# Layer 0's product: ScalarE's quarter in moving blocks of 512 columns, projection one piece sooner

## The chip, the cores and the metric

The kernel runs on one core of a Trainium2 chip. A core has several engines with a queue each: TensorE (matrix products, written PE in the profile, its weight loads PEld), VectorE (DVE), ScalarE (ACT), GpSimd (POOL) and SyncE (SP, which only issues transfers here). They run side by side and wait for each other through semaphores. The metric is the device time of one execution, in microseconds (us). Three runs of the kernel before gave 768.58, 769.27 and 770.39 us, so the median is 769.27 us.

## The reference

The input x has 8 batches of 2048 nodes with 64 channels; adj is a 2048 x 2048 matrix over the nodes. There are two layers, each with a residual and a layer normalization. What matters here is layer 0, a graph convolution whose weights differ from node to node:

```python
w = jnp.einsum('nd,dkio->nkio', embedding, weight)      # d: 16, k: 3, i and o: 64
b = jnp.einsum('nd,do->no', embedding, bias)
As = [eye, A, 2.0 * (A @ A) - eye]
x_g = jnp.einsum('knm,bmc->bnkc', jnp.stack(As, 0), x)
out = jnp.einsum('bnki,nkio->bno', x_g, w)
return out + b
...
x = _layernorm(x + _L0_gnn_ref(x, adj, ...), axis=-1)
x = _layernorm(x + _L1_gnn_ref(x, adj, adj, ...), axis=-1)
```

Layer 1 is a second graph convolution with weights that all nodes share. It begins with a projection of the normalized output h of layer 0, and then multiplies by adj again.

## The kernel before, in words

The kernel goes through three large stages: two multiplications by adj that give the hop and the second hop of x (up to 227 us), layer 0's product with the normalization and the projection (227 to 534 us), and the multiplications by adj of layer 1 (the rest). Only the second of these is changed, with the loop that runs it (lines 834 to 867) and the function `mix0` (line 394).

**The tiles.** The 2048 nodes are 16 tiles of 128 nodes (`NT`, `P`). A tile has 512 columns: 8 batches by 64 channels. The loop over t handles layer 0's product of tile t, the operands for tile t + 1, and what follows for tile t - 1: its normalization and its projection.

**The product.** It swaps the order of the sums in the reference: TensorE first multiplies the features of a tile with `weight` for each embedding entry d, and the result is then scaled, node by node, with the embedding and summed over the 16 entries. A matmul takes as stationary operand the transposed features of one batch (64 channels by 128 nodes) and as moving operand the weights of four embedding entries (64 by 4 x 64 = 256 columns). Two batches lie on rows 0 to 63 and 64 to 127, and their matmuls follow each other as a pair. To keep float32 precision the features and the weights are split into a high, a low and a mixed part (`tt[k][n]`, `w_parts[n][k]`), so that with three k there are nine products to be summed per result.

The loop in `mix0` makes eight blocks per tile: g (two groups of four batches) by dg (four groups of `DG` = 4 embedding entries). A block is 2 x 3 x 3 x 2 = 36 matmuls into one `bank("pm")`, a tile of two PSUM banks. There are four such tiles (line 74), which pm, the transposes (pt) and the projection (pu) share in turn; the next user of one waits until its last reader is done.

**Taking the blocks out.** For six blocks VectorE does it: per embedding entry one `scalar_tensor_tensor` of 128 x 256 (line 431), which multiplies with the embedding column and adds to `acc`. For two blocks (dg = 0 of both g, a quarter of the tile) ScalarE does it: four `activation` of 128 x 256 (line 429) into the tile `aside`. GpSimd sums them in `summed` (line 403) and adds the sum to `acc` in `add_aside` (line 400). In the last tile ScalarE takes two blocks of each g (`on_act` = 2). `aside` comes from the pool `rawp` (five buffers), which also holds parts of the second hop.

**The work between the blocks.** The dictionary `at` says which work is issued ahead of which block (g, dg). Every engine works off its queue in the order of issue (`ordered`). The steps are:

- `of_x`, `of_hop`, `of_second` make the operands of tile t + 1 with `parts` (line 309), three steps each: the high part on ScalarE (line 312), the low part on VectorE (line 314), the mixed part on ScalarE and GpSimd (lines 319 and 320). `of_hop` begins with TensorE transposes (line 300). The input of `of_x` is loaded by SP in `operands` (line 702).
- n1, n2, n3 are the later steps of `layernorm` (line 359) of tile t - 1: square on ScalarE (line 353); square sums, variance (`ln_v`, line 334) and square root (`ln_sd`, line 336); then reciprocal root on VectorE (lines 339, 342, 343 and 345) and scaling on GpSimd (line 374). Ahead of them stand the sums, the mean and the subtraction (lines 362, 363, 365).
- `transpose(h, "hT")` and `project(t - 1, ...)` (line 443): eight transposes, and eight matmuls on `v`, whose results ScalarE copies to z (line 460).
- `times_r(t + 2)` scales the second hop on GpSimd (line 692), and `begin_sum(t + 1)` prepares the next `acc` on GpSimd (line 387).

In the last tile the first steps of layer 1 (`early`) take the place of the next tile's operands.

Of the kernel before, what the change touches and what calls it, by code (L numbers as in the profile page):

```python
# [9 lines left out]
F32 = mybir.dt.float32  # L10
# [3 lines left out]
AF = mybir.ActivationFunctionType  # L14
ALU = mybir.AluOpType
# [3 lines left out]
P = 128  # L19
B, N, C = 8, 2048, 64  # L20
NT = N // P
D = 16
DG = 4
# [16 lines left out]
def pattern(  # L40
# [22 lines left out]
    nc = tc.nc  # L63
# [7 lines left out]
    rawp = pool(ctx, "fraw", RAW)  # L71
# [12 lines left out]
    def bank(name):  # L84

        return psum.tile([P, 2, 512], F32, tag="ps", name=name)
# [40 lines left out]
    def ordered(ins):  # L127
        if in_order:
            tc.keep_in_program_order(ins)
# [173 lines left out]
    def transpose(src, tag, pt=None):  # L303

        tt = xcpool.tile([P, B // 2, P], F32, tag="ln_xc", name=tag)
        ordered(nc.scalar.copy(by_half(tt), transposed(src, pt)))
        return tt
# [75 lines left out]
    def begin_sum(t):  # L383

        acc = work.tile([P, B, C], F32, tag="acc", name="acc")
        for g in range(2):
            ordered(nc.gpsimd.tensor_tensor(
                acc[:, 4 * g : 4 * g + 4, :].rearrange("p (j i) c -> p j i c", j=2),
                bc(0, t)[:, 4 * g : 4 * g + 4, :].rearrange("p (i j) c -> p j i c", j=2),
                ebias[:, t : t + 1, :].unsqueeze(1).to_broadcast([P, 2, 2, C]), ALU.add,  # L390
            ))
        return acc

    def mix0(t, tt, acc, at, on_act=1):

        aside = [None, None]

        def add_aside(g):
            part = acc[:, 4 * g : 4 * g + 4, :]
            ordered(nc.gpsimd.tensor_tensor(part, part, aside[g][:, 0], ALU.add))  # L400

        def summed(one, other, n):
            ordered(nc.gpsimd.tensor_tensor(one[:, :n], one[:, :n], other, ALU.add))  # L403

        for g in range(2):
            part = acc[:, 4 * g : 4 * g + 4, :]
            for dg in range(D // DG):
                if (g, dg) == (1, 2 if on_act == 1 else 0):
                    add_aside(0)
                for work_here in at.get((g, dg), ()):  # L410
                    work_here()
                ds = slice(dg * DG, (dg + 1) * DG)
                pm = bank("pm").rearrange("p j (i d c) -> p j i d c", i=2, d=DG)
                for i in range(2):
                    for k in range(3):
                        for n in range(3):
                            for j in range(2):
                                q = slice(j * C, (j + 1) * C)
                                nc.tensor.matmul(  # L419
                                    pm[:, j, i], lhsT=tt[k][n][q, 2 * g + i, :], rhs=w_parts[n][k][q, ds, :],  # L420
                                    start=(k == 0 and n == 0), stop=(k == 2 and n == 2),
                                )
                if dg < on_act:
                    to = rawp.tile([P, DG, B // 2, C], F32, tag="raw", name="aside")
                for d in range(DG):
                    dd = dg * DG + d
                    got, e = pm[:, :, :, d, :].rearrange("p j i c -> p (j i) c"), emb_sb[:, t, dd : dd + 1]
                    if dg < on_act:
                        ordered(nc.scalar.activation(to[:, d], got, AF.Copy, scale=e))  # L429
                    else:  # L430
                        ordered(nc.vector.scalar_tensor_tensor(part, got, e, part, ALU.mult, ALU.add))  # L431
                if dg < on_act:
                    if dg == 0:
                        aside[g] = to
                    else:
                        summed(aside[g], to, DG)
                    if dg == on_act - 1:
                        for n in (2, 1):
                            summed(aside[g], aside[g][:, n : 2 * n], n)
        add_aside(1)  # L440
        return layernorm(acc)

    def project(t, hT, pus=None):


        for g in range(2):
            pm = bank("pu") if pus is None else pus[g]
            for i in range(2):
                for j in range(2):
                    q = slice(j * C, (j + 1) * C)  # L450
                    nc.tensor.matmul(  # L451
                        pm[:, j, i * 3 * C : (i + 1) * 3 * C], lhsT=hT[q, 2 * g + i, :], rhs=v[q],
                        start=True, stop=True,
                    )
            got = pm[:, :, : 6 * C].rearrange("p j (i k c) -> p j i k c", i=2, k=3)

            order = ["p (i j) c -> p j i c", "p (j i) c -> p j i c", "p (j i) c -> p j i c"]
            to = [bc(k, t)[:, 4 * g : 4 * g + 4, :].rearrange(order[k], j=2) for k in range(3)]
            for k in range(3):
                ordered(nc.scalar.copy(to[k], got[:, :, :, 2 - k, :]))  # L460
# [228 lines left out]
    def times_r(t):  # L689
        to = z2[:, t, :].rearrange("p (j n) -> p j n", n=P)  # L690
        r = rrow[:, t * P : (t + 1) * P].unsqueeze(1).to_broadcast([P, B // 2, P])
        ordered(nc.gpsimd.tensor_tensor(to, to, r, ALU.mult))  # L692
# [9 lines left out]
    def operands(t, quick=False):  # L702

        xt = work2.tile([P, B // 2, P], F32, tag="t0", name="xt")
        load(nc.sync, xt, xT[t])
        tt = [None] * 3

        def begin(k, src):
            where, tag = ((rawp, "raw"), (spool, "s"))[k != 2]
            high = hpool.tile([P, B // 2, P], F32R, tag="hl", name="hl")  # L710
            pair = where.tile([P, 2, B // 2, P], F32R, tag=tag, name="parts")
            tt[k] = [high, pair[:, 0], pair[:, 1]]
            return parts(src, tt[k], by_half if k == 1 else lambda to: to, quick)

        def of_x():
            yield from begin(0, xt)

        def of_hop(pt=None):
            yield from begin(1, transposed(z[1][t], pt))

        def of_second():
            yield from begin(2, by_pair(z[2][t]))

        return tt, of_x(), of_hop, of_second()
# [94 lines left out]
    def early(i, *kinds):  # L819

        got = third_got.setdefault(i, {})
        for lead, part in sorted(third[i], key=lambda part: -part[0]):
            if part.__name__ in kinds:
                part(got)
        third[i] = [part for part in third[i] if part[1].__name__ not in kinds]

    def go(it):
        return lambda: next(it)

    y, s = ("y_high", "y_low"), ("load_sum", "operands")  # L830
    acc, h, norm = first_tile[5], None, None
    tt = first_tile[0]
    coming = operands(1)
    for t in range(NT):
        got, last = {}, t == NT - 1
        at = {(g, dg): [] for g in range(2) for dg in range(D // DG)}
        n1, n2, n3 = [lambda: next(norm)] * 3 if t else [nothing] * 3

        if not last:
            following, of_x, of_hop, of_second = coming  # L840
            of_hop = of_hop()
            at[0, 1] += [go(of_x)] * (1 if t else 3)
            at[0, 2] += [go(of_hop), n1, go(of_hop), go(of_hop), n2]
            if t + 2 < NT:
                at[0, 2] += [lambda: times_r(t + 2)]
                at[1, 0] += [lambda: got.update(coming=operands(t + 2))]
            at[0, 3] += [n3, go(of_second), lambda: got.update(acc=begin_sum(t + 1))]
            at[1, 0] += [go(of_second), go(of_second)]
            at[1, 3] += [lambda: got.update(hT=transpose(h, "hT"))] if t else []
        else:  # L850
            at[0, 1] += [n1, lambda: early(0, *y, *s)]
            at[0, 2] += [n2, lambda: early(1, *y, *s)]
            at[0, 3] += [n3, lambda: early(2, *y)]
            at[1, 0] += [lambda: early(3, *y)]
            at[1, 1] += [lambda: early(4, *y)]
            at[1, 2] += [lambda: got.update(hT=transpose(h, "hT"))]
            at[1, 3] += [lambda: project(t - 1, got["hT"])]
        norm_now = mix0(t, tt, acc, at, 2 if last else 1)
        if 0 < t < NT - 1:
            project(t - 1, got["hT"])  # L860
        if "coming" in got:
            coming = got["coming"]
            next(coming[1])
            next(coming[1])
        norm = norm_now
        h = next(norm)
        if not last:
            tt, acc = following, got["acc"]
# [480 lines left out]
```

## Time and profile before

| what | value |
|---|---|
| median of three runs | 769.27 us |
| the profiled execution | 768.76 us, of which the span is 767.0 us |
| TensorE, matmul | 757.0 us busy, 99% |
| VectorE | 582.8 us busy, 76% |
| ScalarE | 387.7 us busy, 51% |
| GpSimd | 252.5 us busy, 33% |
| granted TensorE clock, mean | 0.997 |
| pm matmuls (line 419), 64 x 256 | 4608, 280 to 286 ns each as recorded |
| line 431, VectorE, 128 x 256 | 376, 483 ns each |
| line 429, ScalarE, 128 x 256 | 136, 475 ns each |
| lines 403 (GpSimd) | 66, 1068 ns each |

The span is the time from the first to the last instruction of the profiled execution. A row of the profile names the line, the engine, the operation, what it writes and reads, the shape and the count; then the busy time and the mean duration of one, and the idle time of the engine ahead of it with what ended that. The two matmuls of a pair run at the same time and matmuls overlap their neighbours, so their pace is read from how many end in a stretch and not from the recorded duration. The chain is the sequence of work that ended last, followed back from the end.

### The profile page before, as it was taken

How to read it: one execution, taken by the hardware profiler on the slowest of the kernel's cores; microseconds unless marked ns; L12 is line 12 of the kernel's file. 1: busy time of each engine (PE TensorE's matmuls, PEld its weight loads, DVE VectorE, ACT ScalarE, POOL GpSimd, SP SyncE). 2: the span in 40 equal slices, each digit the busy share in tenths (PEclk: the TensorE clock that was granted, in tenths of full speed). 3: DMA queues.
4: the chain of work that ended last, by engine and by line, in shares of the span. 5: the costliest groups of instructions: out<-in, count | busy, mean ns of one | idle time of the engine just before them, and what ended most of it. 6: DMA issues, size and time to landing. Idle time of an engine off the chain costs nothing.

```text
span 767.0 us, 18011 instructions
## 1 busy us (share of the span) xinstructions
PE 757.0 (99%) x7246; PEld 674.8 (88%) x7246; DVE 582.8 (76%) x1222; ACT 387.7 (51%) x760; POOL 252.5 (33%) x247
## 2 busy tenths in 40 slices
PE   8999999999999999999999999999999999999996
PEld 6888888888889999999999999998888888888886
DVE  6778766677758898888889888876688648668664
ACT  4446533878744555555545555547787763112111
POOL 0000000000026777777777777766100000012341
PEclk9999999999999999999999999999999999999998
DMA  8998996555510000000000000002354444565731
GB/s 308 374 389 294 340 313 209 164 168 164 171 60 27 20 8 19 20 17 16 17 16 10 20 17 3 3 29 70 127 168 146 138 149 137 178 183 164 217 128 45
DMA packets 73546, 96.77 MB, mean 126 GB/s; under 512 B 4848, under 2 KB 48368, under 8 KB 73328
## 3 DMA queue, kind: packets, MB, share of 16 engines
q1 hardware_dynamic: 62048, 76.66, 30.7%
q10 hardware_dynamic: 11408, 18.89, 6.6%
q8 instruction: 59, 0.97, 0.5%
q14 instruction: 31, 0.25, 0.1%
HBM read 76.65 MB, written 18.87 MB: 125 GB/s over the span
## 4 chain that ended last, share of the span: by engine, by line
PE 96%; DVE 2%; DMA 1%; ACT 1%; POOL 0%; issue 0%; SPq 0%; POOLq 0%; DVEq 0%
PE pm L419 35%; PE accT L641 27%; PE acc L254 15%; PE a L254 10%; PE accT L254 6%; PE pu L451 2%; DMA raw<-in_adj 1%; PE pt L300 1%; DVE acc L431 1%; PE accT L791 1%; DVE hl L238 0%; PE accT L451 0%; ACT aside L429 0%; SPq L123 0%; POOL xc L365 0%
## 5 line engine op out<-in xcount | busy, mean ns | idle before, releaser
L419 PE MATMUL pm<-wh,hl 64*128 64x256 f32 x1536 | 235.4, 286 | 0.7 <-DVE acc L431 0.7
L419 PE MATMUL pm<-wm,parts 64*128 64x256 f32 x1536 | 230.9, 280 | 0.0
L419 PE MATMUL pm<-wl,parts 64*128 64x256 f32 x1536 | 230.8, 280 | 0.0
L641 PE MATMUL accT<-s,hl 128*128 128x512 f32 x896 | 205.7, 390 | 0.0
L431 DVE SCALAR_TENSOR_TENSOR acc<-pm,pack_sb,acc 128x256 f32<-128x256 f32 x376 | 181.5, 483 | 27.5 <-PE pm L419 14.1
L641 PEld LDWEIGHTS accT<-s,hl 128*128 128x128 f32 x896 | 167.6, 188 | 35.4 <-issue 0.2
L419 PEld LDWEIGHTS pm<-wh,hl 64*128 64x128 f32 x1536 | 160.3, 188 | 1.2 <-PE pt L300 0.8
L419 PEld LDWEIGHTS pm<-wl,parts 64*128 64x128 f32 x1536 | 160.2, 188 | 0.0
L419 PEld LDWEIGHTS pm<-wm,parts 64*128 64x128 f32 x1536 | 160.0, 187 | 0.0
L629 ACT CAST s<-raw 128x1024 fp32r<-128x1024 bf16 x104 | 109.7, 1055 | 38.0 <-ACT hl L234 24.7
L254 PE MATMUL acc<-hl,s 128*128 128x512 f32 x512 | 117.3, 390 | 0.6 <-DVE s L223 0.6
L254 PEld LDWEIGHTS acc<-hl,s 128*128 128x128 f32 x512 | 95.8, 188 | 21.8 <-issue 1.0
L692 POOL TENSOR_TENSOR z<-z,rrow 128x512 f32<-128x512 f32 x16 | 21.1, 1319 | 213.0 <-DVE z L665 213.0
L429 ACT ACTIVATE aside<-pm,pack_sb 128x256 f32<-128x256 f32 x136 | 53.3, 475 | 54.0 <-PE pm L419 54.0
L234 ACT CAST hl<-z 128x256 fp32r<-128x256 f32 (+1 forms) x96 | 47.4, 511 | 63.4 <-PE acc L254 24.7
L403 POOL TENSOR_TENSOR aside<-aside 128x512 f32<-128x512 f32 (+2 forms) x66 | 70.5, 1068 | 18.4 <-ACT aside L429 15.7
L254 PE MATMUL a<-hl,s 128*128 128x512 f32 (+1 forms) x352 | 73.4, 370 | 0.0
L254 PEld LDWEIGHTS a<-hl,s 128*128 128x128 f32 x352 | 61.9, 188 | 11.3
L238 DVE TENSOR_TENSOR hl<-z,hl 128x512 fp32r<-128x512 f32 (+1 forms) x96 | 54.6, 576 | 14.0 <-ACT hl L234 11.4
L320 POOL TENSOR_TENSOR parts<-parts 128x512 fp32r<-128x512 f32 x45 | 57.7, 1294 | 11.6 <-DVE parts L314 9.8
L287 POOL TENSOR_TENSOR z<-z,got 128x512 f32<-128x512 f32 x3 | 4.8, 1622 | 143.8 <-ACT got L286 143.8
L254 PE MATMUL accT<-hl,s 128*128 128x512 f32 x192 | 44.3, 390 | 0.0
(129 smaller groups left out, 822.9 us busy)
## 6 DMA issues: line engine op xcount, KB each, us to landing
raw<-in_adj SPq DMA_DIRECT2D x59, 512.0 KB, 5.6
raw<-sums_of SPq DMA_DIRECT2D x64, 256.0 KB, 2.7
sums_of<-z ACTq DMA_DIRECT2D x16, 512.0 KB, 6.1
raw<-quarters SPq DMA_DIRECT2D x32, 256.0 KB, 2.7
raw<-in_adj SPq DMA_DIRECT2D x16, 384.0 KB, 3.0
quarters<-seen ACTq DMA_DIRECT2D x16, 256.0 KB, 5.7
xt<-in_xT SPq DMA_DIRECT2D x16, 256.0 KB, 2.6
z<-in_x SPq DMA_DIRECT2D x15, 256.0 KB, 6.9
```

Source lines behind the costliest of these rows:

```text
L234: ordered(nc.scalar.copy(to[0], src))
L238: ordered(nc.vector.tensor_tensor(to[1], src, to[0], ALU.subtract))
L254: nc.tensor.matmul(accs[i], lhsT=s[:, i * P : (i + 1) * P], rhs=hl[h], start=(first and h == 0), stop=(last and h == 1),)
L320: ordered(nc.gpsimd.tensor_tensor(mixed, mixed, low, ALU.add))
L403: ordered(nc.gpsimd.tensor_tensor(one[:, :n], one[:, :n], other, ALU.add))
L419: nc.tensor.matmul(pm[:, j, i], lhsT=tt[k][n][q, 2 * g + i, :], rhs=w_parts[n][k][q, ds, :], start=(k == 0 and n == 0), stop=(k == 2 and n ...
L429: ordered(nc.scalar.activation(to[:, d], got, AF.Copy, scale=e))
L431: ordered(nc.vector.scalar_tensor_tensor(part, got, e, part, ALU.mult, ALU.add))
L451: nc.tensor.matmul(pm[:, j, i * 3 * C : (i + 1) * 3 * C], lhsT=hT[q, 2 * g + i, :], rhs=v[q], start=True, stop=True,)
L629: ordered(nc.scalar.copy(s, got["raw"]))
L641: nc.tensor.matmul(acc[i][:, c], lhsT=hl[h][:, i * P : (i + 1) * P], rhs=S[:, c * 512 : (c + 1) * 512], start=(kk == 0 and h == 0), stop=( ...
L692: ordered(nc.gpsimd.tensor_tensor(to, to, r, ALU.mult))
```

## The change

ScalarE's quarter is cut another way. Before it was the first four embedding entries of all eight batches (one block of each g). Now it is the first eight embedding entries of the first four batches, g = 0: two blocks (`by_batch`), one per pair of batches, each with moving operands of 8 x 64 = 512 columns, 18 matmuls instead of 36. ScalarE takes such a block out with eight `activation` of 128 x 2 x 64. The remaining blocks (`by_four`) are made and taken out as before. So in all tiles but the last g = 0 has two ScalarE blocks and two VectorE blocks, and g = 1 has four VectorE blocks. In the last tile both g have two of each, as before.

GpSimd's additions for the aside now stand in one place, in `add_aside`, which is issued where `at` holds a number: a 1024-wide, a 512-wide and a 256-wide addition and the one to `acc`, once per tile instead of twice 512, 256 and one to `acc`.

The work between the blocks is distributed anew: hop's first step comes ahead of x's last one, the normalization steps come a block later or earlier, the next tile's load, `times_r` and `begin_sum` come later, and the transpose of h and the projection come one block sooner, so that the projection stands ahead of the last block of its tile instead of after it.

```diff
-    def mix0(t, tt, acc, at, on_act=1):
-
-        aside = [None, None]
+    def mix0(t, tt, acc, at, on_act):
+
+        def block(pm, lhsT, ds):
+            for k in range(3):
+                for n in range(3):
+                    for j in range(2):
+                        q = slice(j * C, (j + 1) * C)
+                        nc.tensor.matmul(
+                            pm[:, j], lhsT=tt[k][n][q, lhsT, :], rhs=w_parts[n][k][q, ds, :],
+                            start=(k == 0 and n == 0), stop=(k == 2 and n == 2),
+                        )
+
+        def e(d):
+            return emb_sb[:, t, d : d + 1]
+
+        def by_batch(g, i):
+            pm = bank("pm").rearrange("p j (d c) -> p j d c", c=C)
+            block(pm, 2 * g + i, slice(0, 2 * DG))
+            if i == 0:
+                aside[g] = [rawp.tile([P, DG, 2, 2, C], F32, tag="raw", name="aside") for _ in range(2)]
+            for d in range(2 * DG):
+                ordered(nc.scalar.activation(aside[g][d // DG][:, d % DG, :, i, :], pm[:, :, d, :], AF.Copy, scale=e(d)))
+
+        def by_four(g, dg):
+            pm = bank("pm").rearrange("p j (i d c) -> p j i d c", i=2, d=DG)
+            for i in range(2):
+                block(pm[:, :, i], 2 * g + i, slice(dg * DG, (dg + 1) * DG))
+            for d in range(DG):
+                part = acc[:, 4 * g : 4 * g + 4, :]
+                got = pm[:, :, :, d, :].rearrange("p j i c -> p (j i) c")
+                ordered(nc.vector.scalar_tensor_tensor(part, got, e(dg * DG + d), part, ALU.mult, ALU.add))
+
+        aside = {}
 
         def add_aside(g):
+            one, other = [a.rearrange("p d j i c -> p d (j i) c") for a in aside[g]]
             part = acc[:, 4 * g : 4 * g + 4, :]
-            ordered(nc.gpsimd.tensor_tensor(part, part, aside[g][:, 0], ALU.add))
-
-        def summed(one, other, n):
-            ordered(nc.gpsimd.tensor_tensor(one[:, :n], one[:, :n], other, ALU.add))
+            for to, more in ((one, other), (one[:, :2], one[:, 2:]), (one[:, 0], one[:, 1]), (part, one[:, 0])):
+                ordered(nc.gpsimd.tensor_tensor(to, to, more, ALU.add))
 
         for g in range(2):
...
+            for n in range(D // DG):
+                for work_here in at.get((g, n), ()):
+                    if isinstance(work_here, int):
+                        add_aside(work_here)
                     else:
-                        ordered(nc.vector.scalar_tensor_tensor(part, got, e, part, ALU.mult, ALU.add))
...
+                        work_here()
+                if g in on_act and n < 2:
+                    by_batch(g, n)
+                else:
+                    by_four(g, n)
         return layernorm(acc)
...
-            at[0, 1] += [go(of_x)] * (1 if t else 3)
-            at[0, 2] += [go(of_hop), n1, go(of_hop), go(of_hop), n2]
+            at[0, 1] += [go(of_hop), n1] + ([] if t else [go(of_x), go(of_x)])
+            at[0, 2] += [go(of_hop), n2, go(of_hop), go(of_x)]
+            at[0, 3] += [n3, go(of_second)]
+            at[1, 0] += [go(of_second), go(of_second)]
+            at[1, 1] += [0]
             if t + 2 < NT:
-                at[0, 2] += [lambda: times_r(t + 2)]
-                at[1, 0] += [lambda: got.update(coming=operands(t + 2))]
-            at[0, 3] += [n3, go(of_second), lambda: got.update(acc=begin_sum(t + 1))]
-            at[1, 0] += [go(of_second), go(of_second)]
-            at[1, 3] += [lambda: got.update(hT=transpose(h, "hT"))] if t else []
+                at[1, 1] += [lambda: got.update(coming=operands(t + 2))]
+                at[1, 2] += [lambda: times_r(t + 2)]
+            at[1, 2] += [lambda: got.update(acc=begin_sum(t + 1))]
+            if t:
+                at[1, 2] += [lambda: got.update(hT=transpose(h, "hT"))]
+                at[1, 3] += [lambda: project(t - 1, got["hT"])]
         else:
             at[0, 1] += [n1, lambda: early(0, *y, *s)]
-            at[0, 2] += [n2, lambda: early(1, *y, *s)]
-            at[0, 3] += [n3, lambda: early(2, *y)]
-            at[1, 0] += [lambda: early(3, *y)]
-            at[1, 1] += [lambda: early(4, *y)]
-            at[1, 2] += [lambda: got.update(hT=transpose(h, "hT"))]
-            at[1, 3] += [lambda: project(t - 1, got["hT"])]
-        norm_now = mix0(t, tt, acc, at, 2 if last else 1)
-        if 0 < t < NT - 1:
-            project(t - 1, got["hT"])
+            at[0, 2] += [n2, n3, lambda: early(1, *y, *s)]
+            at[0, 3] += [lambda: early(2, *y)]
+            at[1, 0] += [0, lambda: early(3, *y)]
+            at[1, 1] += [lambda: early(4, *y), lambda: got.update(hT=transpose(h, "hT"))]
+            at[1, 2] += [lambda: project(t - 1, got["hT"])]
+            at[1, 3] += [1]
+        norm_now = mix0(t, tt, acc, at, (0, 1) if last else (0,))
```

More of the change, by code (lines that the diff above doesn't have):

```diff
@@ L405, in mix0 @@
         for g in range(2):
[L406 to L429, printed above, removed]
-                    else:
-                        ordered(nc.vector.scalar_tensor_tensor(part, got, e, part, ALU.mult, ALU.add))
[L432 to L439, printed above, removed]
@@ L440, in mix0 @@
-        add_aside(1)
+            for n in range(D // DG):
+                for work_here in at.get((g, n), ()):
+                    if isinstance(work_here, int):
+                        add_aside(work_here)
+                    else:
+                        work_here()
[3 more added lines that the diff above has]
+                    by_four(g, n)
         return layernorm(acc)
```

## The prediction

> **What bounds the kernel now.** I read the page first: TensorE is busy 99% of the span, and the chain that ended last is 96% TensorE, with layer 0's product (line 419) its largest part.
>
> ```profile
> PE 96%; DVE 2%; DMA 1%; ACT 1%; POOL 0%; issue 0%; SPq 0%; POOLq 0%; DVEq 0%
> ```
>
> Then I read the chain in order of time through layer 0. From tile 1 to tile 14 it repeats every 19.14 us and holds nothing but TensorE:
>
> ```profile
> 364.18 10.85 PE pm L419 x180
> 375.03 0.24 PE pt L300 x8
> 375.27 2.20 PE pm L419 x36
> 377.47 1.30 PE pu L451 x16
> 378.77 4.31 PE pm L419 x72
> 383.08 0.24 PE pt L300 x8
> ```
>
> Five blocks of 36 matmuls take 10.85 us, so a block takes 2.17 us and one pair (rows 0-63 and 64-127 at once) 120.6 ns. The same view has 100 full-height matmuls of 512 columns in 22.66 us, 226.6 ns each. At the 2.4 columns per ns that the difference between the two fits closely, both carry some 13.5 ns on top.
>
> The margin behind that chain decides, so I read the timelines of VectorE and GpSimd over one tile and an early one:
>
> ```profile
> 367.24 0.17 DVE L334 SCALAR_TENSOR_TENSOR ln_v<-ss,eps 128x8 f32<-128x8 f32 x1
> 369.28 0.19 DVE L339 RECIPROCAL ln_r<-ln_sd 128x8 f32<-128x8 f32 x1
> 369.51 0.42 DVE L342 SCALAR_TENSOR_TENSOR ln_q<-ln_r 128x8 f32<-128x8 f32 x1
> 369.97 0.17 DVE L343 TENSOR_TENSOR ln_q<-ln_q,ln_v 128x8 f32<-128x8 f32 x1
> ...
> 252.27 1.14 DVE L334 SCALAR_TENSOR_TENSOR ln_v<-ss,eps 128x8 f32<-128x8 f32 x1
> ```
>
> ```profile
> 368.60 1.30 POOL L692 TENSOR_TENSOR z<-z,rrow 128x512 f32<-128x512 f32 x1
> ...
> 252.09 2.54 POOL L320 TENSOR_TENSOR parts<-parts 128x512 fp32r<-128x512 f32 x2
> ```
>
> An eight-column step of 0.17 us takes 0.42 us at 369.51 and ends at 369.93, just after GpSimd's instruction ends (369.90). At 252.27 it takes 1.14 us and ends at 253.41; GpSimd's instruction that began at 252.09 ends at 253.38, and GpSimd's next one has by then begun. So such a step waits for the whole GpSimd instruction in progress. VectorE is busy 16.15 us of the 19.14 us tile, so it has 3.0 us to lose.
>
> **What the Trainium skill says.** "SBUF — State Buffer", section "Who interferes with whom": a VectorE instruction with two SBUF inputs and a GpSimd instruction that reads SBUF exclude each other, and whichever starts first keeps the port for its whole instruction. The trace agrees (above). "TensorE: Matmul & The Clock Gate", section "Back-to-back issue gap": an isolated matmul takes N/2.4 + 2.5 ns. The trace has about 11 ns more for both widths, and is used. "ScalarE: Activation LUTs", section "What ACT_TABLE_LOAD costs": 0.833 ns per column. Four aside instructions of 256 columns take 1.57 us here, the last 0.475, so they follow each other every 0.365 us.
>
> **The change, part by part.**
>
> *Matmuls.* A new 512-column block is 9 pairs. No row shows such a pair; by the full-height row a pair takes 226.6 ns, the block 2.04 us against 2.17. Bounds: 9 x 213 = 1.92 us (no fixed part), 9 x 241 = 2.17 us (no gain). I take 2.04, because the fixed part is alike in both rows: 0.13 us per block, 2 blocks in 15 tiles and 4 in the last, so 3.9 + 0.5 = 4.4 us. An undisturbed tile would be 18.88 us.
>
> *ScalarE.* Eight instructions of 256 columns become sixteen of 128. Not shown: bounds 0.20 us (the square root of eight columns occupies ScalarE 0.21) and 0.365. I take 0.365 - 128 x 0.833 ns = 0.26 us, an estimate; eight take 2.07 us. ScalarE is half idle, so the 1.2 us added per tile cost nothing themselves; what they delay is next.
>
> *The order.* VectorE's six blocks per tile now stand together, V2 to V7, after B0 and B1. ScalarE's queue is now B0's eight, hop's high part, the square, B1's eight, the square root, and only then the mixed parts of hop and x. Formerly these mixed parts came ahead of the square root, and GpSimd had finished both sums (line 320) before line 342 arrived. Now both sums land on VectorE's reciprocal-root steps. I walk a tile from the start of B0 with the distances between starts that the three engines' timelines show for the tile at 364: VectorE's block 1.95 us (2.08 in a row of several), a low part 0.60, sums 0.72, mean 0.17, square sums 0.71, reciprocal 0.23; ScalarE's hop high 0.48, square 0.53, mixed part 0.62; GpSimd's subtraction 1.04 and a sum of parts 1.25 to 1.29.
>
>
> - TensorE: B0 ends at 2.04, hop's transposes 2.28, B1 4.32, V2 6.49, V3 8.66, V4 10.83, V5 13.00, transposes of h 13.24, V6 15.41, projection 16.71, V7 18.88.
> - VectorE: previous V7 evicted 1.99; x low part (0.61) 2.60; sums and mean 3.49. GpSimd subtracts until 4.66. ScalarE: B0 done 4.15, hop high 4.63, square to 5.3. VectorE: hop low 5.27, square sums 6.06, ln_v 6.15, V2 evicted 6.53 to 8.48, reciprocal 8.71.
> - ScalarE: B1 5.2 to 7.27, square root 7.5, hop mixed 8.1. GpSimd: hop's sum from 8.2 to 9.5, x's sum to 10.75, back to back.
> - VectorE at 8.71: line 342 waits to 9.5. Line 343 arrives 0.04 us later, x's sum has begun, and it waits to 10.75. Together 2.0 us. V3 evicted at 12.98, second hop's low part 13.58, V4 15.66, V5 17.74, V6 19.82.
>
> By the waits in the built program the projection needs V4's bank, V7 needs V5's, and the next B0 needs V6's. So the projection moves from 15.41 to 15.69 (ends 16.99), V7 waits to 17.77 and ends at 19.94. Behind V7's matmuls the whole TensorE queue stands, the next tile too. GpSimd's four additions for the aside (2.40 + 1.30 + 0.74 + 0.75), now in one run after second hop's sum, then push its last two jobs to 3.0 us into the next tile, where they hold x's low part 0.29 us: 20.23 us from then on. Against 19.14: 0.80 once and 1.09 in 13 tiles, +15.0. Tile 0 has no normalization to wait on: -0.26.
>
> *The projection's move* brings 0 itself: h's transposes need GpSimd's scaling, done at 12.3, and start at 13.00. ScalarE's six copies (1.6 us) end before x's high part is needed. Without that cover it would add up to 0.7 us per tile. The later GpSimd jobs (next sum, scaling by r) have their readers over 3 us later. The xt loads move on SP behind no other load, and have most of a tile to land (2.6 us).
>
> *The last tile* took 20.85 us (512.86 to 533.71), 1.6 of it waiting (TensorE is busy 18.40 of the 20 us from 510 to 530). New: 18.38 undisturbed, but V2's eviction stands behind the reciprocal root, which now waits for two aside batches and two casts (about 9.6), and the low parts of layer 1 around V3 (line 238) wait for the 1024-wide and then the 512- and 256-wide addition. V3 is free near 15.4, the projection and two blocks follow: 21. I count 0, +-1.
>
> Sum: 768.76 (span 767.0 and 1.8 around it) + 15.0 - 0.3 = 783.5 for the profiled execution; the median of before is 0.5 above its profiled one, so 784.0.
>
> **Rivals.**
>
> 1. *The stall never forms, and the matmul gain arrives whole.* If ScalarE and GpSimd drift so that line 342 to 345 pass ahead of the two sums, VectorE ends V5 before 16.7 and every tile is 18.88: 769.27 - 4.4 = 764.9. For it: VectorE has slack in sum, and before too GpSimd and VectorE slid past each other (line 334 took 1.14 us early, 0.17 later). Against it: hop's sum would have to start over half a microsecond later than walked, which 0.32 us per aside instruction would give.
> 2. *Only one step waits*, 0.8 or 1.25 us, and the last GpSimd jobs add 0 to 0.3. V7 then waits 0 to 0.6, the tile is 18.9 to 19.5; with 19.4 the time is 769.27 + 14 x 0.26 = 773. It needs hop's and x's sums apart, for which ScalarE's queue gives no reason.
> 3. *The change does not do what it says*: a 512 pair costs two 256 pairs and the stall is absent. Then 769, within 0.2%. Against it is the 226.6 ns row.
>
> The sign turns on the wait of lines 342 to 345, 2.0 us in the walk. Up to 1.0 us per tile V5 still ends by 16.75 and nothing is lost; up to 1.26 the stall only eats the 0.26 gained; beyond that every tile is longer than before.
>
> **How the numbers follow.** Both steps wait: 0.62, 784, its own range 776 to 790 (aside instruction 0.22 to 0.30, lock of the last GpSimd jobs or not, last tile +-1). One step: 0.12, 768 to 776. No stall: 0.20, 763.5 to 767.7. No difference, within 0.2% (which is about what a measurement of this kernel can tell): 0.05; the last 0.01 is beyond. Range 764.4 to 789.5: it cuts some 0.09 off the fast case and some 0.08 off the slow one. Faster 0.20, same 0.05, slower 0.75.
>
> **What would show it.** In the changed profile: a pm row of 64x256 and one of 64x512, whose block takes 2.04 us. Lines 342 and 343 with means near 0.9 and 1.3 us in layer 0. A wait of TensorE's product for VectorE's acc, over 0.7 us in each of tiles 1 to 14, ahead of V7. A tile of 20.2 us. It is wrong if the chain through layer 0 is all TensorE at 18.9 us, or if TensorE waits for ScalarE or GpSimd instead.

## The result, and the profile after

The changed kernel takes 782.88 us (median of 6 runs, 782.71 to 784.3) against 769.17 us for the kernel before on the same chip (6 runs): the ratio is 1.018, with a 95% interval of 1.0167 to 1.0193. The profiled execution took 782.88 us with a span of 781.1 us, 14.1 us more than before. In the changed file the matmuls of pm are line 403, VectorE's eviction line 426, ScalarE's aside line 417, the additions of the aside line 434, the projection line 457, GpSimd's `begin_sum` line 387 as before; lines 300 to 374 kept their numbers.

First the chain that ended last, by engine. VectorE, 2% of it before, is 7% of it now:

```profile
PE 90%; DVE 7%; ACT 1%; issue 1%; POOL 0%; DVEq 0%; POOLq 0%
```

Then the same chain in order of time through one tile of layer 0 (start, duration, what):

```profile
382.53 0.49 DVE acc L426
383.03 0.04 issue
383.07 4.59 PE pm L403 x54
387.66 0.24 PE pt L300 x8
387.90 10.77 PE pm L403 x162
398.67 0.24 PE pt L300 x8
398.91 2.21 PE pm L403 x36
401.12 0.48 DVE acc L426
...
403.20 4.59 PE pm L403 x54
```

Before, this stretch was all TensorE and repeated every 19.14 us. Now V7 starts at 383.07 and again at 403.20, 20.13 us later, and ahead of each start stand VectorE's evictions of one block (V5). The projection, which lies between 401.1 and 402.7, is hidden in that wait. The piece of 10.77 us holds B1 and four blocks of VectorE; with 2.17 us for each of the four, B1's 512-column block takes 2.09 us.

The waits of TensorE in the whole of layer 0 (us in total, times, longest) say the same for its weight loads, 0.8 us per tile, and its matmuls, 0.5 us:

```profile
PEld pm L403 <- DVE acc L426: 10.9, 14, 0.8
PE pm L403 <- DVE acc L426: 7.9, 16, 0.7
```

The groups of instructions between 240 and 505 us, 13 tiles from tile 1 on, with shapes kept apart, in part (count | busy, mean ns | idle before and what ended it):

```profile
L403 PE MATMUL pm<-wh,hl 64*128 64x256 f32 x950 | 149.7, 285 | 6.7 <-DVE acc L426 6.7
L417 ACT ACTIVATE aside<-pm,pack_sb 128x128 f32<-128x128 f32 x208 | 56.6, 397 | 50.9 <-PE pm L403 50.9
L403 PE MATMUL pm<-wh,hl 64*128 64x512 f32 x156 | 35.0, 417 | 0.0
L343 DVE TENSOR_TENSOR ln_q<-ln_q,ln_v 128x8 f32<-128x8 f32 x13 | 15.8, 1216 | 0.4
L342 DVE SCALAR_TENSOR_TENSOR ln_q<-ln_r 128x8 f32<-128x8 f32 x13 | 7.5, 580 | 0.4
```

The 512-column blocks are there, and it is the 256-column ones that wait. Lines 342 and 343, two steps of eight columns that took 0.17 us where nothing held them, take 0.58 and 1.22 us. The timelines of VectorE and of GpSimd over one tile show on what:

```profile
394.26 0.19 DVE L339 RECIPROCAL ln_r<-ln_sd 128x8 f32<-128x8 f32 x1
394.48 0.56 DVE L342 SCALAR_TENSOR_TENSOR ln_q<-ln_r 128x8 f32<-128x8 f32 x1
395.08 1.21 DVE L343 TENSOR_TENSOR ln_q<-ln_q,ln_v 128x8 f32<-128x8 f32 x1
396.32 0.17 DVE L345 SCALAR_TENSOR_TENSOR ln_r<-ln_q,ln_r 128x8 f32<-128x8 f32 x1
```

```profile
393.72 2.55 POOL L320 TENSOR_TENSOR parts<-parts 128x512 fp32r<-128x512 f32 x2 [3.55 <-ACT parts L319]
```

GpSimd's two sums, 1.3 us each, run from 393.72 to 396.27. Line 342 ends with the first of them, line 343 with the second. This is the exclusion that the Trainium skill states on the page "SBUF — State Buffer", section "Who interferes with whom"; the traces here agree, even for steps of eight columns.

The kernel before had such waits too. Its rows of the same stretch:

```profile
L314 DVE TENSOR_TENSOR parts<-z,hl 128x512 fp32r<-128x512 f32 x13 | 15.7, 1210 | 0.0
L314 DVE TENSOR_TENSOR parts<-xt,hl 128x512 fp32r<-128x512 f32 x14 | 12.9, 918 | 5.0 <-ACT hl L312 5.0
L334 DVE SCALAR_TENSOR_TENSOR ln_v<-ss,eps 128x8 f32<-128x8 f32 x14 | 8.2, 585 | 0.5
L342 DVE SCALAR_TENSOR_TENSOR ln_q<-ln_r 128x8 f32<-128x8 f32 x14 | 5.4, 386 | 0.5
```

Over the 0.69 us of a low part (line 314) and the 0.17 us of a small step that nothing holds, these are 0.52, 0.23, 0.42 and 0.22 us, together 1.4 us per tile: nearly what lines 342 and 343 wait now (0.41 and 1.05). Yet TensorE waited for none of it in this stretch. So the sum of the waits did not grow by much; what differs is how much waiting the order can take where the waits fall, and the experiments measure that for the new order.

**Where the 14 us went.** In both traces I take the start of the first pm matmul, of the hop's transposes in each tile (4.41 us after the tile's start before, 2.19 after) and of the last pm matmul. Layer 0's product grew from 306.63 to 321.09 us, by 14.46:

| part | before | after | difference |
|---|---|---|---|
| tile 0 | 17.57 | 17.40 | -0.17 |
| tile 1 | 19.23 | 20.92 | +1.69 |
| tiles 2 to 13, each | 19.15 | 20.13 | 12 x 0.98 = +11.77 |
| tile 14 and the last | 40.02 | 41.19 | +1.17 |

So the loss is one microsecond in each regular tile. Tile 1 is worse, because there line 342 arrives just after the first sum began and takes 1.15 us instead of 0.56 (line 343: 1.22).

### The profile page after: what moved, and what is told of

Same layout as the page of the kernel before. It is cut to its first block, busy times and chain, and to the rows that moved or that the text cites. A ratio compares the mean times of both kernels' runs of the same rounds, so it can differ in the third digit from the quotient of the medians.

```text
span 781.1 us, 16921 instructions
## 1 busy us (share of the span) xinstructions
PE 763.3 (98%) x6634; PEld 668.4 (86%) x6634; DVE 585.0 (75%) x1222; ACT 403.0 (52%) x896; POOL 252.9 (32%) x217
## 4 chain that ended last, share of the span: by engine, by line
PE 90%; DVE 7%; ACT 1%; issue 1%; POOL 0%; DVEq 0%; POOLq 0%
PE pm L403 31%; PE accT L647 26%; PE acc L254 15%; PE a L254 9%; DVE acc L426 6%; PE accT L254 6%; PE pt L300 1%; PE accT L797 1%; PE first L143 1%; ACT aside L417 1%; DVE ln_q L343 0%; PE pu L457 0%; DVE ln_q L342 0%; PE accT L457 0%; ACT sq L353 0%
## 5 line engine op out<-in xcount | busy, mean ns | idle before, releaser
L403 PE MATMUL pm<-wh,hl 64*128 64x256 f32 (+1 forms) x1332 | 222.8, 304 | 7.9 <-DVE acc L426 7.9
L403 PE MATMUL pm<-wm,parts 64*128 64x256 f32 (+1 forms) x1332 | 217.6, 296 | 0.0
L403 PE MATMUL pm<-wl,parts 64*128 64x256 f32 (+1 forms) x1332 | 217.5, 296 | 0.0
L403 PEld LDWEIGHTS pm<-wh,hl 64*128 64x128 f32 x1332 | 144.8, 187 | 13.9 <-DVE acc L426 10.9
L403 PEld LDWEIGHTS pm<-wm,parts 64*128 64x128 f32 x1332 | 144.7, 187 | 1.6
L403 PEld LDWEIGHTS pm<-wl,parts 64*128 64x128 f32 x1332 | 144.9, 187 | 1.3
L417 ACT ACTIVATE aside<-pm,pack_sb 128x128 f32<-128x128 f32 x272 | 74.1, 396 | 64.3 <-PE pm L403 64.3
L434 POOL TENSOR_TENSOR aside<-aside 128x1024 f32<-128x1024 f32 (+2 forms) x51 | 74.8, 1466 | 3.0 <-ACT aside L417 0.4
L466 ACT COPY z<-pu 128x256 f32<-128x256 f32 x90 | 26.3, 400 | 36.8 <-PE pu L457 36.8
```

What stands on the lines that cost most here:

```text
L403: nc.tensor.matmul(pm[:, j], lhsT=tt[k][n][q, lhsT, :], rhs=w_parts[n][k][q, ds, :], start=(k == 0 and n == 0), stop=(k == 2 and n == 2),)
L417: ordered(nc.scalar.activation(aside[g][d // DG][:, d % DG, :, i, :], pm[:, :, d, :], AF.Copy, scale=e(d)))
L434: ordered(nc.gpsimd.tensor_tensor(to, to, more, ALU.add))
```

## The experiments

The question was whether the wait of lines 342 and 343 for GpSimd is the cause of the microsecond, or whether the new order itself (six VectorE blocks in a row, their PSUM banks, the projection ahead of V7) stalls the tile. The kernels e1 to e4 ran together, then e5 to e8, then e9 and e10; the kernel before ran beside each group (medians 769.24, 769.46 and 769.37 us), and each ratio below is to it, with its 95% interval. Every tile time below is the mean distance of the hop's transposes over tiles 2 to 13.

### e1: without the three steps

The edit in part:

```diff
     ordered(nc.vector.reciprocal(r0, sd))
+    if short:
+        yield r0
+        return
```

In layer 0's normalization the refinement of the reciprocal root (lines 342, 343 and 345) is left out; the rough reciprocal is used as it is.

> The changed kernel without lines 342, 343 and 345 in layer 0's normalization: the reciprocal of the square root is used as it comes, its refinement is left out. Theory (the two steps wait for GpSimd's sums of parts, and V3 to V5 are late by that): 0.5 us of own work and some 1.6 us of waits go from VectorE's path in each of tiles 1 to 14, V5 is out before V7 is due, the tile falls to 18.9 to 19.2 us and the time to 765 to 770 us. Rival (six VectorE blocks in a row with the projection ahead of the last one leave too few banks, whatever the steps wait for): only the 0.5 us of own work is gained per tile, 774 to 777 us.

Measured: 766.09 us, ratio 0.9958 (0.9941 to 0.9975). The chain of this kernel, in order of time, is all TensorE again (its matmuls and its projection stand three lines lower in the file, at 406 and 460):

```profile
392.83 1.27 PE pu L460 x15
394.10 4.26 PE pm L406 x54
398.36 0.24 PE pt L300 x8
398.60 10.77 PE pm L406 x162
409.37 0.24 PE pt L300 x8
409.61 2.20 PE pm L406 x36
411.81 1.27 PE pu L460 x15
```

The tile is 18.98 us from one projection to the next. That is what the changed order costs when TensorE isn't held up: 0.17 us less than before. VectorE is not quite free even here: the second hop's low part takes 0.94 us against 0.69, and nothing is lost by it. By itself e1 can't tell the wait from the work: the steps' own 0.17 us each go as well.

### e2 and e3: the sums moved behind the root

```diff
 # e2: only x's mixed part behind n3
-at[0, 2] += [go(of_hop), n2, go(of_hop), go(of_x)]
-at[0, 3] += [n3, go(of_second)]
+at[0, 2] += [go(of_hop), n2, go(of_hop)]
+at[0, 3] += [n3, go(of_x), go(of_second)]
 # e3: hop's and x's
+at[0, 2] += [go(of_hop), n2]
+at[0, 3] += [n3, go(of_hop), go(of_x), go(of_second)]
```

> Only the mixed part of x is issued after the reciprocal root instead of before it; hop's stays. Theory: line 342 still waits 0.4 us for hop's sum, line 343 no longer waits its 1.05 us; the second hop's low part may meet the moved sum (0 to 0.5 us). Tile 19.0 to 19.5 us, time 767 to 774 us. Rival (banks alone): no change, 783 us.

> The mixed parts of hop and x are both issued after the reciprocal root. Theory: neither 342 nor 343 waits; but GpSimd's whole queue of the tile then runs later (scaling by r and the next sum at its end), so that these reach further into the next tile and hold x's low part and the mean by up to 1.3 us. Tile 18.9 to 19.6 us, time 766 to 775 us. Rival (banks alone): no change, 783 us.

Measured: e2 774.86 us, 1.0074 (1.0057 to 1.0091), a tile of 19.53; e3 771.48 us, 1.0027 (1.0017 to 1.0038), a tile of 19.35. Nothing is left out in these two; only places change. Each sum that no longer meets the root gives time back, but e2 missed its range (767 to 774 us), and neither reaches e1. The rows of VectorE say why. In e2 line 343 is back at 0.17 us; the moved sum now meets the second hop's low part instead:

```profile
L314 DVE TENSOR_TENSOR parts<-z,hl 128x512 fp32r<-128x512 f32 x13 | 14.5, 1118 | 0.0
L342 DVE SCALAR_TENSOR_TENSOR ln_q<-ln_r 128x8 f32<-128x8 f32 x13 | 7.7, 589 | 0.4
L343 DVE TENSOR_TENSOR ln_q<-ln_q,ln_v 128x8 f32<-128x8 f32 x13 | 2.2, 167 | 0.4
```

In the changed kernel that low part takes 0.68 us. In e3 line 342 is free too (0.17 us), but the low part takes 1.12 us as in e2, and the multiplication of the mean meets `begin_sum`:

```profile
L363 DVE TENSOR_TENSOR s<-s,part 128x8 f32<-128x8 f32 x14 | 9.4, 671 | 0.5
```

### e4: two more GpSimd steps in other places

```diff
-at[0, 2] += [go(of_hop), n2]
-at[0, 3] += [n3, go(of_hop), go(of_x), go(of_second)]
+at[0, 2] += [go(of_hop), n2, times_r(t + 2)]
+at[0, 3] += [n3, begin_sum(t + 1), go(of_hop), go(of_x), go(of_second)]
```

(on top of e3, with both steps taken from their former place ahead of V6; the calls of `times_r` and `begin_sum` are written short here and in e5)

> As the third, and scaling by r and the next sum are issued where the kernel before had them (ahead of and just after the reciprocal root), in time that GpSimd is idle. Theory: no wait of 342 and 343, and nothing of GpSimd's queue in the way of x's low part; only the second hop's low part meets the next sum (0.6 us). Tile 18.9 to 19.1 us, time 764.5 to 768 us, faster than the kernel before. Rival (banks alone): no change, 783 us.

Measured: 770.9 us, 1.0017 (1.0009 to 1.0025), a tile of 19.22: outside what was expected. Lines 342, 343 and 363 are all free (0.17 us), and one wait is left, at the second hop's low part:

```profile
L314 DVE TENSOR_TENSOR parts<-z,hl 128x512 fp32r<-128x512 f32 x13 | 16.6, 1277 | 0.0
```

That is 0.59 us over 0.69, and TensorE still waits 0.2 us per tile. So the wait hadn't been removed; it had been moved from one VectorE instruction to the next.

### e5: the low part where GpSimd is idle

```diff
-at[0, 3] += [n3, begin_sum(t + 1), go(of_hop), go(of_x), go(of_second)]
-at[1, 0] += [go(of_second), go(of_second)]
+at[0, 3] += [go(of_second), n3, go(of_second), begin_sum(t + 1), go(of_hop), go(of_x)]
+at[1, 0] += [go(of_second)]
```

> As e4, but the second hop's high and low parts stand ahead of V3 (the low part right behind the reciprocal root, where GpSimd is idle) instead of behind it. Theory: what was left in e4 is one more wait for GpSimd, 0.59 us at the second hop's low part (1.27 us against 0.68), of which VectorE's slack of about 0.35 us covers a part and 0.2 us per tile comes through. With no sum in progress where it now stands, the low part takes 0.7 us, V7 no longer waits, and the tile is the 18.98 us of e1: 14 x 0.23 = 3.2 us less than e4, about 767 (765.5 to 768.5), faster than the kernel before. Rival: the order of six VectorE blocks in a row has no slack for the root and a low part together, whatever GpSimd does; then V3 is as late as in e4, the tile stays at 19.2 and the time at 770 to 772.

Measured: 767.95 us, 0.9978 (0.9969 to 0.9986), a tile of 18.98, as expected. VectorE does the same work as in the changed kernel, and none of it between V2 and V4 is held:

```profile
L314 DVE TENSOR_TENSOR parts<-z,hl 128x512 fp32r<-128x512 f32 x14 | 9.6, 686 | 0.0
L342 DVE SCALAR_TENSOR_TENSOR ln_q<-ln_r 128x8 f32<-128x8 f32 x14 | 2.4, 168 | 0.5
L343 DVE TENSOR_TENSOR ln_q<-ln_q,ln_v 128x8 f32<-128x8 f32 x14 | 2.3, 168 | 0.5
```

With this the order of the blocks does not stall the tile by itself: six blocks in a row, the banks, the projection ahead of V7 and the 512-column blocks are all in e5, and its tile is shorter than before. The waits by themselves cost nothing either, as the kernel before shows with its 1.4 us. The loss takes both: an order with little room, and waits that fall into it.

### e10: sums half as long

```diff
-ordered(nc.gpsimd.tensor_tensor(mixed, mixed, low, ALU.add))
+ordered(nc.gpsimd.tensor_tensor(mixed[:, :n], mixed[:, :n], low[:, :n], ALU.add))   # n: half for hop and x
```

The changed kernel in its own order; half of hop's and of x's mixed part goes without its low part.

> The changed kernel with GpSimd's two sums of the hop's and of x's mixed parts over half their columns (256 instead of 512; the other half of each mixed part goes without its low part): same instructions, same order, same places. Theory (a VectorE step waits until GpSimd's instruction in progress ends, so the wait is as long as what is left of the sums): the sums take about 0.74 us each by the 256-column rows of GpSimd, the pair ends 1.1 us sooner, and lines 342 and 343 wait about 0.4 to 0.7 us together instead of 1.45. Less the 0.3 us of slack that the runs so far show, 0.1 to 0.4 us per tile stay, so 9 to 14 us less than the changed kernel: 769 to 774. Rival (the order of the six VectorE blocks, the banks or the number of GpSimd's instructions stalls the tile, not their length): 781 to 784.

Measured: 770.56 us, 1.0018 (1.001 to 1.0026), a tile of 19.23.

```profile
L320 POOL TENSOR_TENSOR parts<-parts 128x256 fp32r<-128x256 f32 x28 | 20.1, 740 | 49.3 <-ACT parts L319 45.7 <-DVE acc L426 3.5
L342 DVE SCALAR_TENSOR_TENSOR ln_q<-ln_r 128x8 f32<-128x8 f32 x14 | 9.3, 666 | 0.5
L343 DVE TENSOR_TENSOR ln_q<-ln_q,ln_v 128x8 f32<-128x8 f32 x14 | 2.8, 203 | 0.5
```

Not an instruction or a place is changed, only the length of two per tile. The first sum is over when line 342 arrives, the second holds it to its end, and line 343 is free. So VectorE's wait is as long as what is left of GpSimd's instruction, and with a shorter wait the tile is shorter.

Put together, with the wait taken as the excess of lines 342, 343 and of the second hop's low part over 0.17, 0.17 and 0.69 us, and the loss as the tile less 18.98:

| kernel | wait, us per tile | tile, us | loss, us |
|---|---|---|---|
| after | 0.41 + 1.05 | 20.13 | 1.15 |
| e2 | 0.42 + 0.43 | 19.53 | 0.55 |
| e4 | 0.59 | 19.22 | 0.24 |
| e10 | 0.50 + 0.03 | 19.23 | 0.25 |
| e5 | 0 | 18.98 | 0 |

In every row with a wait the loss is the wait less 0.3 us, within 0.1. (x's low part, which comes before these blocks, is not counted: it takes 0.95 us in e4 and 0.96 in e5, and e5 loses nothing by it. e3 waits in part ahead of V2, where VectorE also waits for TensorE, and isn't in the table.) The slack that VectorE has between V2 and V5 in the new order, the waiting that costs TensorE nothing, is therefore 0.3 us per tile.

### e7: the matmul part by itself

```diff
-block(pm, 2 * g + i, slice(0, 2 * DG))
+for half in (slice(0, DG), slice(DG, 2 * DG)):
+    block(pm[:, :, half], 2 * g + i, half)
```

(on top of e5)

> As e5, but each 512-column block is computed as two blocks of 256 columns (36 pairs of matmuls become 18 pairs twice as often: the same bank, the same readers). It measures the matmul part of the change alone, on a tile in which nothing else stalls TensorE. Theory, by the trace of the changed kernel (2.09 us a block against 2.17): 0.08 x (2 x 15 + 4) = 2.7 us more than e5, or 0.16 us per tile. The figure of the prediction, 0.13 us per block, would give 4.4 us more; rival 3 of the prediction (no gain) gives the same time as e5.

Measured: 770.06 us, 1.0009 (1.0 to 1.0017), 2.1 us more than e5 from the same group; a tile of 19.15, 0.17 more than e5. So a 512-column block saves 0.08 us, not 0.13. The last tile is alike in e5 and e7 within 0.1 us, since it waits for other things, so what arrives is 15 x 0.17 = 2.5 us at most.

### e8: the projection put back

```diff
-at[1, 2] += [lambda: got.update(hT=transpose(h, "hT"))]
-at[1, 3] += [lambda: project(t - 1, got["hT"])]
+at[1, 3] += [lambda: got.update(hT=transpose(h, "hT"))]
 ...
+if 0 < t < NT - 1:
+    project(t - 1, got["hT"])
```

> The changed kernel with only the projection put back behind V7, and h's transposes back ahead of V7. The prediction gave this move 0 us, worked out without a stall. In the stalled tile theory now says otherwise: V7 waits for VectorE to leave V5's bank, 17.9 us after B0's start, whatever stands ahead of it, and the projection (1.2 us of TensorE) fills a part of that wait; put behind V7 it comes on top: 14 x 1.2 = 16 us more than the changed kernel, 795 to 800. Rival, the prediction's 0 as it stands: 782 to 784, because VectorE also gains time while the projection runs and all six of its blocks follow the same 1.2 us sooner relative to TensorE.

Measured: 783.51 us, 1.0175 (1.0158 to 1.0192), a tile of 20.10. My revised theory of 16 us falls; the prediction's 0 holds. The product's rows of e8 show where the wait is now:

```profile
L403 PE MATMUL pm<-wh,hl 64*128 64x256 f32 x962 | 151.6, 283 | 1.3 <-DVE acc L426 0.9
L403 PE MATMUL pm<-wh,hl 64*128 64x512 f32 x156 | 34.3, 421 | 5.8 <-DVE acc L426 5.8
```

In the changed kernel the 256-column row waited 6.7 us and the 512-column row nothing. Without the projection ahead of it V7 takes the next PSUM tile in turn, the one that V4 leaves, starts at once, and the projection follows when V5's is free. Then the next tile's B0 waits for V6's. I had kept V7's bank fixed and moved only the projection. What moves ahead also takes the tile that comes free earlier, and the wait comes out one user later with about the same length. How much the move brings in a tile without a stall was not run.

### e6 and e9: the last tile

The last tile waits too, before and after. Both are built on e5 and move the first steps of layer 1 in the last tile: e6 behind the reciprocal root, e9 also those between V2 and V3 behind V3.

```diff
 # e6
-at[0, 1] += [n1, lambda: early(0, *y, *s)]
-at[0, 2] += [n2, n3, lambda: early(1, *y, *s)]
-at[0, 3] += [lambda: early(2, *y)]
-at[1, 0] += [0, lambda: early(3, *y)]
+at[0, 1] += [n1]
+at[0, 2] += [n2, n3, lambda: early(0, *y, *s)]
+at[0, 3] += [lambda: early(1, *y, *s), lambda: early(2, *y)]
+at[1, 0] += [lambda: early(3, *y), 0]
 # e9, on e6
-at[0, 3] += [lambda: early(1, *y, *s), lambda: early(2, *y)]
-at[1, 0] += [lambda: early(3, *y), 0]
+at[1, 0] += [lambda: early(1, *y, *s)]
+at[1, 1] += [lambda: early(2, *y), 0, lambda: early(3, *y)]   # then early(4, *y) as before
```

> As e5, and in the last tile the two early casts and the early low part of layer 1 stand behind the reciprocal root instead of ahead of it, and the first half's four additions one low part later. Theory: in the last tile V2's eviction stands behind the root, and the root behind 1.35 us of casts on ScalarE and behind B1's eviction; without the casts the root comes about 1.1 us sooner, and with the 1024-wide addition behind the low part the wait of 1.2 us there is gone: 1 to 2 us less than e5, 764.5 to 766. Rival: the last tile is bounded by ScalarE's four aside batches and casts in sum, so what is moved is waited for later: same as e5 within 0.5 us.

> As e6, and in the last tile the early low parts of layer 1 that stood between V2 and V3 stand behind V3's eviction. Theory: in e6 the two low parts of layer 1 between V2 and V3 took 3.1 us, most of it waiting for GpSimd's additions, and V3's bank was free only then; moved behind V3 they let V3's bank go 2 to 3 us sooner, and the last tile comes down from 21.6 to between 19 and 20: 1.5 to 2.5 us less than e5, 765.5 to 766.5. Rival: the last tile is set by ScalarE's four aside batches and their banks; then the time stays at e5's and e6's 768 to 769.

Measured: e6 769.3 us, 0.9993 (0.9983 to 1.0003); e9 767.18 us, 0.9969 (0.996 to 0.9979), the lowest median of the complete kernels here; its ratio and that of e5 lie within each other's intervals. From the hop's transposes of tile 14 to the last pm matmul it is 38.20 us in e5, 38.40 in e6 and 37.21 in e9. e6 shows nothing gained: as soon as the root came sooner, two low parts of layer 1 between V2 and V3 took 3.09 us together, most of it behind GpSimd's additions of the aside:

```profile
520.74 3.09 DVE L238 TENSOR_TENSOR hl<-z,hl 128x256 fp32r<-128x256 f32 x2
```

e9 takes that out and gains 1.0 us there, less than the 1.5 to 2.5 expected, because the projection then waits up to 1.9 us for ScalarE's copy of hT. e6's median is 1.4 us above e5's, more than the 0.2 us of its profile: six of its 12 runs took 767.8 to 768.8 us, the profiled one among them, and six 769.8 to 770.3. Why, stays open.

## Why the prediction was right, and where its steps were off

The time (784.0 against 782.88) and the mechanism (both steps wait for GpSimd's two sums, V7 then waits for V5's bank) came out as predicted; that the sum came so close is in part luck, since several of its steps were off in opposite directions. By its steps, with times from B0's start in the tile that begins at 385.33:

- **What would show it.** The rows of 64x256 and 64x512, the long means at lines 342 and 343, and a wait of pm for acc ahead of V7 are all there; the means are 0.58 and 1.22 us (0.9 and 1.3 predicted). The tile is 20.13 us (20.2 predicted).
- **The matmuls.** 2.09 us per 512-column block, not 2.04, and 0.17 us per tile (e7), not 0.26. The premise that the fixed part is alike for all rows failed: the pairs follow each other every 0.231 us, and not every 226.6 ns.
- **ScalarE.** The eight aside instructions of B0 take 2.17 us and the mean of one is 0.40, so they follow each other every (2.17 - 0.40) / 7 = 0.25 us; 0.26 was estimated.
- **The wait.** GpSimd's sums end at 9.69 and 10.94 (9.5 and 10.75 predicted). Line 342 arrives at 9.15 and not at 8.71, because V2's eviction starts at 6.96 and not at 6.53: by their pace its matmuls end near 6.7, later with the longer blocks, and the eviction begins some 0.25 us after that, where the walk had 0.04. So the wait is 1.46 us. The predicted 2.0 held 0.34 us of the two steps' own time, which leaves 1.66; the other 0.2 is the later arrival less the later sums.
- **The threshold.** "Up to 1.0 us nothing is lost" is the step that failed. The runs show 0.3 us. The 1.0 counted the steps' own 0.34 us as wait, and the later V2 took another 0.4 of it; TensorE's own 18.98 for 18.88 gives 0.1 back. This error and the too long wait are one error seen twice: a late VectorE waits less, and has less to lose. V7's start was hit all the same, 17.87 against 17.77, because it follows from when GpSimd's second sum ends, and not from when line 342 arrives. The sign turns at 0.3 + 0.17 = 0.47 us of wait and not at 1.26; e10 and e4, with 0.53 and 0.59, are slower than before.
- **Rival 2** would have been mispriced by that: with one step waiting 0.8 to 1.25 us it said 773 with the tile at 19.4; e2, with 0.85 us in all, has 19.53 and 774.86.
- **GpSimd's last jobs** were to hold x's low part for 0.29 us and so to make 20.23 of 19.94. They don't: x's low part takes 0.73 us against 0.69. In the tile shown it starts 0.11 us ahead of the second addition of `begin_sum`, and it is GpSimd's addition that is held (1.2 us, where the first takes 0.75). The 0.19 us between 19.94 and 20.13 are V7's later start (0.10) and the distance from V7's first matmul to the next B0's, 2.26 us for 2.17. That 20.13 came out so near 20.23 is thus luck in part: the predicted hold is absent, and 0.19 us that the walk didn't have stand in its place.
- **The sum.** +15.0 was predicted for tiles 1 to 14; with tile 14 at the 0.98 of the others it is 1.69 + 13 x 0.98 = 14.4. Tile 1 was to lose the least, 0.80, and lost the most; the others were to lose 1.09 each and lost 0.98, so the two misses cancel in part. Tile 0 gave 0.17 (0.26 predicted), and the last tile lost 0.2 (0 predicted).
- **The projection's move** brings 0, as predicted, in the stalled tile (e8).
- **Rival 1** (no stall) is what e5 is, with 18.98 us for the tile and not 18.88: it would have been 767 to 768, and not 764.9. Rival 3, that the 512-column blocks save nothing, is refuted by e7.
- **The margin.** "VectorE has 3.0 us to lose" was read from its idle time in a whole tile. The room on the way to V7 is 0.3 us.

## What to carry to other kernels

When steps are moved between queues, list for each VectorE instruction with two SBUF inputs which GpSimd instruction is in progress when it arrives: its wait is what is left of that one, however small the step is, and a step right behind it may wait for GpSimd's next. It goes the other way too: a GpSimd instruction that comes second is held. Moving the GpSimd work moves the wait to the next such instruction (e2, e3, e4), so the place to look for is one where GpSimd is idle anyway (e5). The sum of the waits does not decide: 1.4 us per tile cost nothing in the kernel before, and 1.46 us cost 1.15 in the changed one. Compare the wait with the slack up to the bank that TensorE needs next, counted from when the chain really starts, and work the slack and the wait out of the same walk.

## What the runs showed of the hardware

- A pair of 64-row matmuls of 512 columns has a pace of 0.231 us, while a full-height matmul of 512 columns has 226.6 ns: 4 to 5 ns more, where I had taken the same.
- How long VectorE's small step waits depends on when it arrives. In tile 1 line 342 came 0.17 us after the first sum's start and waited 1.0 us; in most later tiles it came 0.76 us after and waited 0.4. Line 343 follows within 0.04 us, finds the second sum begun, and waited 1.05 us in all of them.
- GpSimd waits in the same way. The additions of `begin_sum` take 0.75 us in the kernel before; in the changed one the second of each pair begins just after x's low part and takes 1.2 us, so that the mean is 0.98 (the first row is of the kernel before, the second of the changed one, both between 240 and 505 us):

```profile
L387 POOL TENSOR_TENSOR acc<-z,ebias 128x256 f32<-128x256 f32 x26 | 18.9, 748 | 0.0
L387 POOL TENSOR_TENSOR acc<-z,ebias 128x256 f32<-128x256 f32 x26 | 24.9, 980 | 0.0
```

- VectorE's evictions, which read PSUM and one SBUF operand, aren't held: in the changed kernel the 184 that run wholly beside one GpSimd instruction take 484 ns on average, and so do the 50 with none beside them.
